# Layer 0 of a two-layer graph attention kernel: h and gate as one 512-column product in fifteen steps

## The chip, the cores and the metric

The kernel runs on one core of a Trainium2 chip. The metric is the device time of one execution in microseconds; the median of the runs counts. All data are 32-bit floats, and the products are made on TensorE (PE) in that type. The other engines are VectorE (DVE), ScalarE (ACT), GpSimd (POOL) and SyncE (SP), whose queue issues every load and store.

## The reference

The input is 128 graphs of 64 nodes with 768 features, and an adjacency mask. Two attention layers follow each other, each with a residual and a layer normalization. The change is in layer 0:

```python
h = einsum('bnd,ade->bane', x, W)              # 12 heads of 64: one 768 x 768 product
th = tanh(h)
attn = (th @ w_src) + (th @ w_dst).T           # per head, a 64 x 64 score of each graph
attn = where(attn >= 0, attn, 0.2 * attn); attn = where(~adj, -999, attn); attn = softmax(attn)
feat = elu(attn @ h + b)
gate = sigmoid(x @ H_w.T + H_b)                # a second 768 x 768 product
x1 = layernorm(x + gate * feat + (1 - gate) * x)
```

Layer 1 is a multi-head attention over x1 with four 768 x 768 products, for queries, keys, values (v) and the output.

## The kernel before

Tokens lie in 64 tiles of 128 (two graphs each), which go through the kernel in 32 pairs. Phase A (`phase_a`) is layer 0 together with the v product of layer 1; phase B is the rest of layer 1.

**Products.** Phase A multiplies a pair by a 768 x 768 matrix with a seven-product scheme: the pair, and the weights, are seen as 2 x 2 blocks of 384, and seven products of blocks (and of sums of blocks) do what eight would. The class `Product` (its matmuls are recorded at L214) does one such product in 7 steps of 3 matmuls, each with 128 x 128 of transposed tokens as the stationary side and 384 weight columns as the moving side. Its three accumulators X, Z and Y are banks of the pool `psX`, which has four. They are evicted partly by an ACT copy (`snap`, L444) and a DVE addition (`into`, L467), partly by a copy alone (L465). The sums of token blocks are four POOL instructions of 384 columns (`token_sums`, L263 to L266), those of weight blocks are made once at the start (`weight_sums`, L178). H_w is transposed at the start by PE (`hw_blocks`, L395).

Phase B uses another scheme for its products, with fifteen steps: 2 x 3 blocks of tokens by 3 x 3 blocks of 256 weights, fifteen products in place of eighteen. The table `STEPS` says for each step which token block or sum and which weight slot it takes, into which of four accumulator chains it goes, and to which of the six output blocks the running sum of the chain is added or subtracted after that step. The class `Stream` (L915) executes a step: two matmuls, and then the reads, the first of a block by `first` and later ones by `add`.

**Stages of a pair.** For a pair, phase A loads x twice (as rows, and as 32 x 32 blocks that DVE transposes, L423), makes h (`start_h`) and gate (`start_g`), and then for each of its two tiles: tanh (L504), a multiplication by w_dst on POOL (L508) and its sum per head on DVE (L511), the same for w_src (L516, L520), the w_dst scores to DRAM and back as rows (`dst_out`, `dst_in`), the other graph's h to the other partitions (`exchange`), scores with Prelu on ACT (L558), mask (L565) and maximum (L569) on DVE, Exp on ACT (L574), scaling on POOL (L584), transposing and aggregating on PE (L595, L613), ELU (`elu`), the mix with the gate (`mix1`, `mix2`: L646, L647, L655, L656), the normalization, and a store of x1. The gate's bias is added by POOL (`gate_in`, L623). Three pairs later x1 comes back, is transposed, and v is made with the third weight matrix.

**Order.** The order of the work is written out by hand: `at(step, f)` puts a piece of work at a step, and `run` issues the steps in order. Each engine executes its instructions in the order of issue. `O[p]` is the step at which pair p's h begins. It is 14 steps per pair for the first pairs, which have no v beside them, and 21 from then on: 7 for h, 7 for gate, 7 for v. A tile's other stages are placed at constants after `O[p]`.

**Weights.** W, H_w and Wv lie with their sums in three tiles, `w0`, `w1` and `w2`. When layer 0 is through, Wq and Wk are loaded into the places of `w0` and `w1`.

Of the kernel before, what the change touches and what calls it, by code (L numbers as in the profile page):

```python
# [20 lines left out]
BIG = 3e38  # L21

# [39 lines left out]
def kernel(  # L62
# [81 lines left out]
    def weight_tile(tag):  # L144
        return wts.tile([P, 7, CH, HALF], F32, name=f"w{tag}", tag=f"w{tag}")
# [3 lines left out]
    def weight15(i):  # L149
        t = wts.tile([P, 7, CH, HALF], F32, name=f"w{i}", tag=f"w{i}").rearrange(  # L150
            "p s c o -> p (s c o)"
        )

        spare[i] = t[:, 15 * 2 * 256 :]
        return t[:, : 15 * 2 * 256].rearrange("p (s c o) -> p s c o", s=15, c=2)
# [98 lines left out]

    PLACE = [(0, 0), (1, 1), (1, 0), (0, 1)]
# [4 lines left out]
    def token_sums(Ss, Ta, Tb):  # L260

        tt = nc.gpsimd.tensor_tensor
        tt(Ss[:, 0], Tb[:, :CH], Tb[:, CH:], ALU.add)  # L263
        tt(Ss[:, 1], Ss[:, 0], Ta[:, :CH], ALU.subtract)
        tt(Ss[:, 2], Ta[:, :CH], Tb[:, :CH], ALU.subtract)
        tt(Ss[:, 3], Ta[:, CH:], Ss[:, 1], ALU.subtract)  # L266

    def run(events, n_steps):
        for g in range(n_steps):
            for f in events.pop(g, []):  # L270
                f()
        assert not events, sorted(events)
# [56 lines left out]
    def phase_a(ctx):  # L329
        k6 = ctx.enter_context(tc.tile_pool(name="k6", bufs=2))  # L330
# [13 lines left out]
        hp = k3.tile([P, 3, D], F32, name="hp")  # L344
        gp = k3.tile([P, 3, D], F32, name="gp")
        h_at = [xb[:, 2], xb[:, 3], hp[:, 0], hp[:, 1], hp[:, 2]]
        g_at = [xb[:, 4], gp[:, 0], gp[:, 1], gp[:, 2]]
# [10 lines left out]
        def load_tile(p, i):  # L358
# [6 lines left out]
        w0 = weight_tile(0)  # L365
        w0_v = w0.rearrange("p s c o -> p s (c o)").rearrange(
            "p s (a c e) -> p s a c e", a=A // 2, e=E
        )
        W_v = W.rearrange("a (h p c) e -> h p a c e", h=2, c=CH)
        for kh, oh in ((0, 0), (1, 0), (0, 1), (1, 1)):  # L370
            nc.sync.dma_start(
                w0_v[:, SLOT[kh, oh]],
                W_v[kh][:, oh * 6 : (oh + 1) * 6],
            )

            if (kh, oh) == (1, 0):
                load_tile(0, 1)
        load_adj(0)
        w1 = weight_tile(1)
        hrows = {}  # L380

        def load_hrow(oc):

            if oc < 3:
                hrows[oc] = gp[:, oc]
            else:
                hrows[oc] = k3.tile([P, D], F32, name=("z", "tmp", "th")[oc - 3])
            nc.sync.dma_start(hrows[oc], H_w[oc * P : (oc + 1) * P, :])

        def hw_blocks(oc):  # L390
            hrow = hrows.pop(oc)
            for kh in range(2):
                ps = psa.tile([P, CH, P], F32, name="pa")
                for c in range(CH):
                    nc.tensor.transpose(ps[:, c, :], chunk0(hrow, kh * CH + c), ident)  # L395
                dst = w1[:, SLOT[kh, oc // CH], :, (oc % CH) * P : (oc % CH + 1) * P]
                nc.scalar.copy(dst, ps)

        for oc in range(NC):
            load_hrow(oc)  # L400
        wd_bc = rows(k3, w_dst.rearrange("a e o -> (a e o)"), "wd_bc")
        ws_bc = rows(k3, w_src.rearrange("a e o -> (a e o)"), "ws_bc")
        b_bc = rows(k3, b, "b_bc")
        hb_bc = rows(k3, H_b, "hb_bc")
        w2 = weight_tile(2)
# [41 lines left out]
        def sums(d):  # L447
            Ss = k6.tile([P, 4, CH, P], F32, name="S")
            token_sums(Ss, *d["T"])
            d["S"] = Ss  # L450
# [9 lines left out]
        def into(tiles):  # L460
            def sink(k, ps, kept):
                i, half = PLACE[k]
                o = tiles[i][:, halves(half)]
                if kept is None:
                    nc.scalar.copy(o, ps)  # L465
                else:
                    nc.vector.tensor_tensor(o, ps, kept, ALU.add)  # L467

            return sink

        def start_h(d):
            d["h"] = [h_at[(2 * d["p"] + i) % 5] for i in range(2)]
            d["W"] = product(d, lambda i, c: w0_v[:, i, :, c, :], into(d["h"]))

        def start_g(d):
            d["g"] = [g_at[(2 * d["p"] + i) % 4] for i in range(2)]
            d["G"] = product(d, lambda i, c: w1[:, i, c, :], into(d["g"]))
# [17 lines left out]
        class Tile0:  # L495
# [5 lines left out]
            def tanh(self):  # L501
                self.h = self.d["h"][self.i]
                self.th = k3.tile([P, D], F32, name="th")
                nc.scalar.activation(self.th, self.h, AF.Tanh)  # L504

            def dst_mul(self):
                self.tmp = k3.tile([P, D], F32, name="tmp")
                nc.gpsimd.tensor_tensor(self.tmp, self.th, wd_bc, ALU.mult)  # L508
# [112 lines left out]
            def gate_in(self):  # L621
                self.g = self.d["g"][self.i]
                nc.gpsimd.tensor_tensor(self.g, self.g, hb_bc, ALU.add)  # L623
# [5 lines left out]
            def elu(self):  # L629

                self.z = k3.tile([P, D], F32, name="z")
# [54 lines left out]

        for c in range(CH):
            at(0, lambda c=c: weight_sums(lambda s: w0_v[:, s, :, c, :], nc.vector, range(3)))

            at(1, lambda c=c: weight_sums(lambda s: w0_v[:, s, :, c, :], nc.vector, [3]))  # L690
            for k in range(4):
                at(
                    13 + 4 * c + k,
                    lambda c=c, k=k: weight_sums(lambda s: w2[:, s, c], nc.gpsimd, [k]),
                )
        for oc in range(NC):
            at(oc // 2 + 2, lambda oc=oc: hw_blocks(oc))

        for k, block in enumerate(((0, 0), (1, 0), (0, 1), (1, 1))):
            at(2 + k, lambda block=block: weight_plain(w2, Wv, [block]))  # L700
# [3 lines left out]


        O = [14 * p if p < 3 else 21 * p - 21 for p in range(NP)]
        for p in range(NP):
            d, o = st[p], O[p]
            d["p"] = p
            if p:  # L710
                at(max(o - 20, 1), lambda p=p: load_adj(p))
                at(o + 10, lambda p=p: load(p))
# [7 lines left out]
            if p:  # L720
                at(max(o - 20, 1), lambda d=d: xb_in(d, 0))
                at(max(o - 16, 1), lambda d=d: xb_in(d, 1))
                at(o - 6, lambda d=d: xT(d, 0))
                at(o - 5, lambda d=d: xT(d, 1))
                at(o - 4, lambda d=d: sums(d))
            else:
                at(0, lambda d=d: d.update(T=[transposed(d["x"][0])]))
                at(1, lambda d=d: d["T"].append(transposed(d["x"][1])))
                at(1, lambda d=d: sums(d))
            at(o, lambda d=d: start_h(d))  # L730
            at(o + 7, lambda d=d: start_g(d))
            for i in range(7):
                at(o + i, lambda d=d, i=i: dense(d, "W", i))
                at(o + 7 + i, lambda d=d, i=i: dense(d, "G", i))
            for i, s in ((1, o), (0, o + (4 if p == NP - 1 else 5))):
                t = Tile0(p, i)
                at(s + 6 + (i == 0), t.tanh, t.cap)
                at(s + 7, t.dst_mul)
                at(s + 8, t.src_mul)
                at(s + 9, t.dst_sum, t.dst_out)  # L740
                at(s + 10, t.src_sum)
                at(s + 13, t.dst_in)
                at(s + 16, t.exchange)

                at(s + (15 if i else 17), lambda t=t: t.add(0))
                at(s + (16 if i else 17), lambda t=t: t.add(1))
                at(o + (14 if i else 16), t.gate_in)
                at(o + (17 if i else 18), t.gate)
                n = s - (i == 1)
                at(n + 18, t.mask, t.top)  # L750
                at(n + 19, lambda t=t: t.exp(0))
                at(n + 20, lambda t=t: t.exp(1))
                (at_front if i else at)(s + 21, lambda t=t: t.scale(0), lambda t=t: t.scale(1))

                n = s - (p == NP - 1 and i == 1)
                at(n + 24, t.probs)
                at(n + 25, t.aggregate)
                at(s + 26, t.elu)
                at(s + 27, t.mix1)
                at(s + 28, t.mix2)  # L760
                at(s + 29, t.norm1)

                n = s + (0 if p == NP - 1 else 1)
                at(n + 30, t.norm2)
                at(n + 31, t.spill)
# [8 lines left out]
            def x1_sums(d):  # L774
                d["T"] = [d["x1T", i] for i in range(2)]
                sums(d)

            if p < NP - 3:
                v = O[p + 3] + 14
                times = ((1, v - 19, v - 13), (0, v - 16, v - 10))  # L780
            elif p < NP - 1:

                v = O[-1] + (21 if p == NP - 3 else 28)
# [503 lines left out]
```

## Time and profile before

| | us |
|---|---|
| median of 3 runs | 2845.72 (2845.65 to 2846.51) |
| span of the profiled execution | 2842.6 |
| end of phase A (the last v matmul ends) | about 1462 |
| DVE busy, share of the span | 65% |
| POOL busy, share of the span | 54% |
| ACT busy, share of the span | 42% |
| HBM read and written | 191.4 and 101.1 MB |

The profile is one execution. Its span goes from the first to the last instruction; the time of a run has some 3 us around it. Busy shares are averages over the two phases, so stages must be looked at for themselves. A matmul of 32-bit floats appears as two records in the trace, each with a weight load beside it. A busy PE says that its queue was full; how long a matmul takes is read from the distance between records in an unbroken stretch.

### The profile page before, as it was taken

The page shows a single profiled execution, that of the slowest core. Times are in us where ns is not written, and L with a number is a line of the kernel's source. Part 1 is how long each engine was busy: PE and PEld are TensorE (multiplying, and loading weights), DVE is VectorE, ACT ScalarE, POOL GpSimd, SP SyncE. Part 2 cuts the span into 40 slices and gives each one's busy share as a digit, 9 for nine tenths or more (in the row PEclk, how much of TensorE's full clock was granted, in tenths as well). Part 3 has the DMA queues.
Part 4 walks back from the last instruction along what each step waited for, and adds up shares of the span by engine and source line. Part 5 has one row for each costly group of instructions (what it writes and reads, how often), then busy time and mean ns, then how long its engine had stood idle before and what let it go on. Part 6 is the DMA issues. An engine that isn't in the chain of part 4 may idle for free.

```text
span 2842.6 us, 50750 instructions
## 1 busy us (share of the span) xinstructions
PE 2805.4 (99%) x18108; PEld 2062.4 (73%) x18108; DVE 1856.1 (65%) x3724; ACT 1199.2 (42%) x3737; POOL 1544.7 (54%) x1653
## 2 busy tenths in 40 slices
PE   8899999999999999999999999999999999999998
PEld 5556565655655656656568888888888888888887
DVE  4887777877878777777774555555555555555556
ACT  4666656566565665656632221222211222211223
POOL 4755656556566555665546545446555456454455
PEclk9999999999999999999999999999999999999999
DMA  5434444344454454544651221212211212211222
GB/s 168 118 115 143 138 136 143 116 139 143 132 146 120 133 151 124 146 126 132 183 186 35 90 71 63 81 58 89 90 66 62 87 57 90 89 64 63 90 84 73
DMA packets 358685, 308.41 MB, mean 108 GB/s; under 512 B 226593, under 2 KB 304161, under 8 KB 358433
## 3 DMA queue, kind: packets, MB, share of 16 engines
q1 hardware_dynamic: 358144, 304.77, 35.2%
q8 instruction: 144, 2.36, 0.4%
q14 instruction: 109, 0.88, 0.1%
q10 hardware_dynamic: 288, 0.39, 0.0%
HBM read 191.41 MB, written 101.06 MB: 103 GB/s over the span
## 4 chain that ended last, share of the span: by engine, by line
PE 91%; DVE 4%; ACT 1%; DMA 1%; POOL 1%; issue 1%; SPq 1%; DVEq 0%; POOLq 0%; ACTq 0%
PE X L915 43%; PE X L214 40%; PE pb L1062 2%; PE pb L980 2%; PE pa L613 2%; PE pa L595 1%; PE pb L1038 1%; DMA s<-dst_d 1%; ACT s L558 0%; POOL Sc L897 0%; ACT s L574 0%; DVE s L565 0%; DVE xb L656 0%; DVE z L646 0%; DVE T L423 0%
## 5 line engine op out<-in xcount | busy, mean ns | idle before, releaser
L214 PE MATMUL X<-w,S 128*128 128x384 f32 x2304 | 796.8, 491 | 10.9 <-DVE v L486 3.1
L214 PEld LDWEIGHTS X<-w,S 128*128 128x128 f32 x2304 | 430.3, 190 | 298.1 <-DVE v L486 4.3
L915 PE MATMUL X<-S,w 128*128 128x256 f32 x2752 | 635.4, 379 | 0.0
L214 PE MATMUL X<-w,T 128*128 128x384 f32 x1728 | 598.6, 489 | 7.4 <-ACT snap L444 6.4
L915 PEld LDWEIGHTS X<-S,w 128*128 128x128 f32 x2752 | 518.1, 190 | 68.0
L214 PEld LDWEIGHTS X<-w,T 128*128 128x128 f32 x1728 | 325.3, 191 | 234.6 <-ACT snap L444 18.5
L958 DVE TENSOR_TENSOR xs<-xs,X 128x256 f32<-128x256 f32 x512 | 209.7, 418 | 175.1 <-PE X L915 167.0
L915 PE MATMUL X<-w,Sc 128*128 128x256 f32 x1280 | 294.4, 381 | 0.1
L574 ACT ACTIVATE s<-s,nmx 128x64 f32<-128x64 f32 x768 | 256.1, 335 | 76.7 <-DVE nmx L569 76.7
L941 DVE TENSOR_TENSOR k<-k,X 128x256 f32<-128x256 f32 x320 | 132.6, 418 | 232.0 <-PE X L915 160.3
L915 PEld LDWEIGHTS X<-w,Sc 128*128 128x128 f32 x1280 | 241.5, 190 | 34.2 <-DVE xs L958 0.9
L941 DVE TENSOR_TENSOR q<-q,X 128x256 f32<-128x256 f32 x320 | 133.0, 419 | 193.4 <-PE X L915 153.9
L915 PE MATMUL X<-xb,w 128*128 128x256 f32 x1024 | 258.0, 382 | 0.4 <-ACT q L936 0.4
L326 ACT ACTIVATE xs<-xs,shift,rstd 128x768 f32<-128x768 f32 x62 | 63.5, 1025 | 436.5 <-POOL shift L322 430.2
L444 ACT COPY snap<-X 128x384 f32<-128x384 f32 x288 | 135.5, 470 | 226.8 <-PE X L214 224.3
L936 ACT ACTIVATE k<-X,bk_c 128x256 f32<-128x256 f32 x192 | 91.0, 474 | 316.1 <-PE X L915 316.1
L508 POOL TENSOR_TENSOR tmp<-th,wd_bc 128x768 f32<-128x768 f32 x64 | 147.8, 2310 | 124.7 <-ACT th L504 124.7
L915 PEld LDWEIGHTS X<-xb,w 128*128 128x128 f32 x1024 | 192.0, 190 | 27.9 <-ACT q L936 0.8
L558 ACT ACTIVATE s<-s,src 128x64 f32<-128x64 f32 x768 | 193.1, 335 | 32.8 <-DMA s<-dst_d 32.8
L936 ACT ACTIVATE q<-X,bq_c 128x256 f32<-128x256 f32 x192 | 91.0, 475 | 273.6 <-PE X L915 273.6
L897 POOL TENSOR_TENSOR w<-cT 128x256 f32<-128x256 f32 x32 | 23.3, 727 | 333.9 <-PE X L915 332.7
L317 POOL TENSOR_TENSOR rstd<-rstd,neg_half 128x1 f32<-128x1 f32 x126 | 69.1, 549 | 232.5 <-DVE rstd L316 232.1
(123 smaller groups left out, 4283.2 us busy)
## 6 DMA issues: line engine op xcount, KB each, us to landing
xb<-in_x_dram SPq DMA_DIRECT2D x64, 384.0 KB
s<-dst_d SPq DMA_DIRECT2D x128, 192.0 KB
x_d<-xb SPq DMA_DIRECT2D x64, 384.0 KB
xT_d<-T SPq DMA_DIRECT2D x64, 384.0 KB
v_d<-v SPq DMA_DIRECT2D x128, 192.0 KB
xb<-xT_d SPq DMA_DIRECT2D x32, 768.0 KB
xb<-v_d SPq DMA_DIRECT2D x256, 96.0 KB
xs<-x_d SPq DMA_DIRECT2D x64, 384.0 KB
```

The costliest lines, as they stand in the source:

```text
L214: nc.tensor.matmul(o, self.lhsT(i, c), rhs, start=first and c == 0, stop=last and c == CH - 1, skip_group_check=True,)
L317: nc.gpsimd.tensor_tensor(rstd, rstd, neg_half, ALU.pow)
L326: nc.scalar.activation(r, r, AF.Identity, bias=shift, scale=rstd)
L444: nc.scalar.copy(t, ps)
L508: nc.gpsimd.tensor_tensor(self.tmp, self.th, wd_bc, ALU.mult)
L558: nc.scalar.activation(self.s[:, a], self.s[:, a], AF.Prelu, bias=self.src[:, a : a + 1], alpha=LEAKY_ALPHA,)
L574: nc.scalar.activation(self.s[:, a], self.s[:, a], AF.Exp, bias=self.nmx[:, a : a + 1], accum_out=self.sm[:, a : a + 1],)
L613: nc.tensor.matmul(self.pos[h2][own, j, :], self.pt[rws, j, own], rhs, start=True, stop=True,)
L915: nc.tensor.matmul(ps, self.lhsT(r, slot, c), self.rhs(r, slot, c), start=start and c == 0, stop=stop and c == 1, skip_group_check=True,)
L936: nc.scalar.activation(o[:, b], ps, AF.Identity, bias=bias[:, hd : hd + 1], scale=1.0 if positive else -1.0)
L941: nc.vector.tensor_tensor(o[:, b], o[:, b], ps, ALU.add if positive else ALU.subtract)
L958: nc.vector.tensor_tensor(o, o, ps, ALU.add if positive else ALU.subtract)
```

## The change

The h and gate products become one product `HG` for most pairs. The weights of both lie side by side in `whg`: fifteen slots of two 128-row chunks with 512 columns, 256 of W and 256 of H_w. A `Stream`, which moves to the top of the kernel, does the fifteen steps for both at once; its accumulators have 512 columns. At the first read of an output block, DVE takes the gate's half, with its bias, and ACT takes h's half; later reads are one DVE addition over both halves.

```diff
+        def start_hg(d, key, parts):
...
+            def first(b, positive, ps):
+                o, ps = at_block(b), view(ps)
+                m = n
+                if lo + n == 2 and HB_EVICT:
+                    nb = b % 3
+                    hb = hb_bc[:, nb * 256 : (nb + 1) * 256]
+                    if positive:
+                        nc.vector.tensor_tensor(o[:, n - 1], ps[:, n - 1], hb, ALU.add)
+                    else:
+                        nc.vector.tensor_tensor(o[:, n - 1], hb, ps[:, n - 1], ALU.subtract)
+                    m = n - 1
+                if m:
+                    nc.scalar.activation(
+                        o[:, :m], ps[:, :m], AF.Identity, scale=1.0 if positive else -1.0
+                    )
+
+            def add(b, positive, ps):
+                o = at_block(b)
+                nc.vector.tensor_tensor(o, o, view(ps), ALU.add if positive else ALU.subtract)
...
             def gate_in(self):
-                self.g = self.d["g"][self.i]
-                nc.gpsimd.tensor_tensor(self.g, self.g, hb_bc, ALU.add)
+                self.g = self.d["hg"][self.i][:, 1]
+                if not HB_EVICT:
+                    nc.gpsimd.tensor_tensor(self.g, self.g, hb_bc, ALU.add)
```

The eleven sums of token blocks are POOL instructions of 256 columns, each in its own buffer:

```diff
+        S1 = [k1.tile([P, 2, P], F32, name=f"S{k}") for k in range(len(SUMS))]
...
+        def block_sum(d, k, eng):
+            r0, r1, op = SUMS[k]
+            eng.tensor_tensor(S1[k], block(d, r0), block(d, r1), op)
```

Pairs 0 and 1 are multiplied plainly, so that they need no sums of weights. Pair 0's h reads W as it is loaded (384 columns at a time), pair 1's h and both gates read blocks of 256 columns, in six matmuls for each block of a tile. ACT spreads W into `whg` (`spread_w`), and `hw_blocks` puts the transposed H_w there; the blocks that a weight sum will overwrite are kept a second time (`kept_at`).

```diff
+        def plain(d, i, half):
+
+            ps = psX.tile([P, HALF], F32, name="X")
+            for k in range(NC):
+                nc.tensor.matmul(
+                    ps.rearrange("p (a e) -> p a e", e=E),
+                    d["T"][i][:, k, :],
+                    w_raw[:, k // CH, half * 6 : (half + 1) * 6, k % CH, :],
+                    start=k == 0,
+                    stop=k == NC - 1,
+                    skip_group_check=True,
+                )
+            (nc.scalar.copy if half else nc.vector.tensor_copy)(d["hg"][i][:, 0, halves(half)], ps)
...
+        def plain_g(d, i, nb):
+
+            ps = psX.tile([P, 256], F32, name="X")
+            for k in range(NC):
+                slot, c = 3 * (k // 2) + nb, k % 2
+                nc.tensor.matmul(
+                    ps,
+                    d["T"][i][:, k, :],
+                    kept_at(slot)[:, c, :] if slot in KEPT else whg[:, slot, c, WH[1]],
...
+        W_ORDER = (1, 4, 5, 0, 8, 2, 3, 6, 7, 9, 10, 11, 12, 13)
...
+        for n, k in enumerate(W_ORDER):
+            at(BEGIN["sums"][n], lambda k=k: weight15_sum(whg, k, nc.vector, slice(0, 512)))
+        for k, part in enumerate(((0, 0), (1, 0), (0, 1), (1, 1))):
+            at(BEGIN["wv"][k], lambda part=part: weight_plain(w2, Wv, [part]))
```

The last pair takes the fifteen steps twice, first for h and then for the gate, with 256 columns. A full pair now has 22 steps, 15 for `HG` and 7 for v, and v comes two pairs behind. Steps are fractions now; a table gives each stage its place (`A_LEAD` for the tile that comes first, `A_TAIL` for the other, `A_PAIR` for the pair's loads and sums), and a long table `MOVED` of corrections is added for the first five and the last three pairs.

```diff
+O_FIRST = (0, 12, 34, 56)
...
-        O = [14 * p if p < 3 else 21 * p - 21 for p in range(NP)]
+        O = list(O_FIRST) + [O_FIRST[-1] + 22 * (p + 1) for p in range(NP - len(O_FIRST))]
+        END = O[-1]
+        V_BASE = O[2:] + [END + 21, END + 30]
...
+            if p < 2:
+                at(0, lambda d=d: places_hg(d))
+                for n in range(6):
+                    i = (n // 3 + p) % 2
+                    if first and n < 4:
+                        at(BEGIN["h0"][n], lambda d=d, n=n: plain(d, n // 2, n % 2))
+                    if p:
+                        at(BEGIN["h1"][n], lambda d=d, i=i, n=n: plain_blocks(d, i, n % 3))
+                    at(BEGIN[f"g{p}"][n], lambda d=d, i=i, n=n: plain_g(d, i, n % 3))
+                dense = []
+            elif last:
+                dense = [("W", o, 0.5, (0,)), ("G", o + 7.5, 0.5, (1,))]
             else:
...
+                dense = [("HG", o, 1, (0, 1))]
...
+            v = V_BASE[p] + 15 + V_MOVED.get(min(p, p - NP, key=abs), 0)
             at(v, lambda d=d: start_v(d))
```

Wq and Wk are loaded at later steps of the last pair, since `whg` lies in both of their places until its last product is done. Phase B is otherwise as before.

## The prediction

> **What bounds the kernel now.** First the page: which engine is full, and whether it stays full.
>
> ```profile
> span 2842.6 us, 50750 instructions
> PE 2805.4 (99%) x18108; PEld 2062.4 (73%) x18108; DVE 1856.1 (65%) x3724; ACT 1199.2 (42%) x3737; POOL 1544.7 (54%) x1653
> ...
> PE   8899999999999999999999999999999999999998
> ...
> PEclk9999999999999999999999999999999999999999
> ```
>
> TensorE is busy in every slice but the first two and the last, at its full clock. A busy PE need not be an efficient one, so I asked next for busy time by stage (PE, PEld, DVE, ACT, POOL, then clock, DMA share, GB/s).
>
> ```profile
> 0.00:50.00 50.00, 39.37 (x135) 24.52 (x136) 25.36 (x43) 13.73 (x27) 13.35 (x17) 0.97 0.70 209
> 50.00:100.00 50.00, 46.08 (x239) 26.90 (x238) 37.23 (x55) 35.73 (x135) 41.40 (x34) 1.00 0.39 95
> 100.00:150.00 50.00, 43.67 (x275) 25.57 (x274) 39.50 (x59) 34.95 (x129) 34.51 (x31) 0.97 0.41 112
> 150.00:200.00 50.00, 46.56 (x285) 27.72 (x284) 43.34 (x67) 32.07 (x108) 30.74 (x29) 0.97 0.42 121
> ...
> 300.00:500.00 200.00, 200.00 (x1059) 120.07 (x1058) 149.06 (x234) 128.14 (x460) 114.82 (x111) 1.00 0.48 140
> 500.00:700.00 200.00, 199.31 (x1056) 119.86 (x1055) 153.85 (x239) 120.97 (x410) 115.60 (x109) 1.00 0.44 129
> ...
> 1400.00:1450.00 50.00, 45.95 (x245) 27.55 (x244) 34.91 (x61) 26.20 (x97) 19.94 (x22) 1.00 0.76 243
> ```
>
> From 200 to 1400 us PE has no gap; 24.3 us are idle before 200 us (10.6, 3.9, 6.3, 3.4) and 4.1 us at the end of layer 0. The chain of waits gives the pitch.
>
> ```profile
> 134.16 9.70 PE X L214 x24
> ...
> 195.05 29.22 PE X L214 x90
> ...
> 227.72 7.94 PE X L214 x24
> ...
> 239.11 29.22 PE X L214 x90
> ...
> 1514.60 2.95 PE pb L980 x96
> ...
> 1579.96 37.32 PE X L915 x172
> ```
>
> One pair of token tiles takes 239.11 - 195.05 = 44.06 us of PE work. A matmul is recorded twice (4032 records of L214 for 32 x 3 products of 21 matmuls). A record of 384 columns takes 29.22/90 = 0.3247 us, one of 256 takes 37.32/172 = 0.217. The time goes with the columns, about 0.1077 us per 128, so I take 0.4324 us for 512, a width this trace doesn't have. Work taken from PE is therefore taken from the time, as long as the others keep up.
>
> **The change on PE.** A pair's h and gate are now 2 x 7 steps x 3 matmuls of 384: 84 records x 0.3247 = 27.27 us. Fifteen steps x 2 matmuls of 512 are 60 x 0.4324 = 25.94. That is 1.33 us a pair, for pairs 2 to 30: -38.6. The last pair's two separate fifteen-step products are 120 x 0.217 = 26.04: -1.2. Pair 0 plainly is 48 x 0.3247 + 72 x 0.217 = 31.21, pair 1 is 144 x 0.217 = 31.25: +3.9 and +4.0. **PE's work: -31.9 us.** The v product, transposes and aggregation keep their counts.
>
> **The change on the others**, from these rows (mean ns after "us,"):
>
> ```profile
> L958 DVE TENSOR_TENSOR xs<-xs,X 128x256 f32<-128x256 f32 x512 | 209.7, 418 | 175.1 <-PE X L915 167.0 <-POOL xs L879 3.0
> ...
> L623 POOL TENSOR_TENSOR gp<-gp,hb_bc 128x768 f32<-128x768 f32 x48 | 87.7, 1839 | 0.0
> ...
> L467 DVE TENSOR_TENSOR gp<-X,snap 128x384 f32<-128x384 f32 x80 | 44.0, 551 | 8.7 <-PE X L214 5.3 <-ACT s L558 3.3
> ```
>
> *DVE* had (149.06 + 153.85)/400 x 44.06 = 33.4 us a pair. Six evictions of 0.55 go (3.3). Ten additions of 512 columns come; from 418 and 551 ns I extend to 686: 6.9 us. Six first evictions of 256 with the gate's bias come: 2.5. So 39.5 of a new pair of 44.06 - 1.33 = 42.7 us, 92%. *POOL* loses the bias, 2 x 1.84, and 4 sums of about 1.1 us; it gets 11 of 0.73 (the 256-wide sums of L897): 8.0 for 8.1, nothing. *ACT* loses 8 copies of 0.47 and gets 6 of 0.47: -0.9. None of this is on PE's path by its sum; only its place in a queue can matter. If that cover failed and DVE became the bound, its 8% of air is 3.2 us a pair.
>
> **Where a queue can bite.** A chain's running sum is read after each step, and the chain's next matmul comes two steps later: 2 x 4 x 0.4324 = 3.46 us for the read. I walked one pair through the changed kernel's instruction order with the rows' durations. The tightest place follows the tail of the previous pair, at the lead tile's aggregation (end: A). DVE has queued there: two z additions (0.93, counting start to start), the other tile's mask (1.10) and maximum (0.87), the gate's first read of step 11 (0.42), a wait for ACT's first read of h (0.55 with its signals), the 512-wide addition (0.6). It ends at A + 4.6; PE wants that bank for step 14 at A + 3 x 1.73 = 5.2. Then mix1 and mix2 stand ahead of the read of step 12, done at A + 7.1, while v's second step wants that bank at A + 8.9. Both fit, the first by 0.6 us. The mask waits for the Prelus, these for a DMA; behind it are PE's banks. From a stall of nothing to 0.5 us a pair I take 0.1: **+3** (0 to +15).
>
> Two rules of the Trainium skill speak against the change. *SBUF — State Buffer*, section "Who interferes with whom": a VectorE operation with two SBUF inputs and a GpSimd one that reads SBUF lock each other out for the whole instruction. The timeline shows it:
>
> ```profile
> 499.72 0.95 DVE L655 SCALAR_TENSOR_TENSOR z<-gp,z 128x768 f32<-128x768 f32 x1
> ...
> 509.53 2.57 POOL L508 TENSOR_TENSOR tmp<-th,wd_bc 128x768 f32<-128x768 f32 x1 [1.94 <-ACT th L504]
> ...
> 510.82 2.10 DVE L655 SCALAR_TENSOR_TENSOR z<-xb,z 128x768 f32<-128x768 f32 x1
> ```
>
> 0.95 alone, 2.10 behind POOL. If each pair's mask met such a lock, 1.15 - 0.6 = 0.55 us would reach PE, +16 in all. But POOL's queue has nothing ready between the x1 sums, done about when the aggregation is, and the scalings, which wait for the exponentials; so I take the uncontended values. *PSUM — Partial Sum Buffer*, "PSUM bank collisions raise a hardware error": two engines must not read one bank of the same partitions at once. Here the first read of each block is split between DVE and ACT in one bank; the order does make ACT wait for DVE. In parallel the pair would take 0.47, in turn 0.42 + 0.47 + signals = 1.0. No row of before has it; it is in the walk above, inside the 3.46 us.
>
> **The start.** Before, PE loses 24.3 us of idle plus a slow clock: 9.70 against 7.94 for 24 records at 134 us, and 4.18 us for the first six (0.70 each): together 28.3. It waits there for the weight sums (DVE needs W, then 12 and 12 sums) and for pairs that follow at 14 steps each. Now the plain products need no sums. By the rows: 5.9 for x, 0.6 for its copy, 2.2 cold, 0.7 for W's second half, whose landing moves from third to fourth in SP's queue. Then 13 us of h, the H_w transposes, and h of pair 1, whose x blocks are no longer followed by Wv in the queue; they land at about 27 us (6.7 + 0.8 MB at 0.35 MB/us from 5 us, rates of the first 30 us), turned at 28.4, wanted at 28.7. The 14 weight sums of 1024 columns (about 1.2 us each, by the 684 ns of a 512-wide DVE sum, L290, extended) lie beside 31 us of gate products. Pair 2 then meets DVE late by about 1.4 us, and POOL with 12 sums of Wv at 1.05 (L178) on top of its own work, perhaps 2; 3.5 for what I missed. That makes 16: **-12** (-17 to 0, if every saved wait returns at pair 2).
>
> **The end.** v of pair 31 needs the last tile's softmax. Before, three v products cover it (13.6 us each), now two, and the last one is held back behind the tail's transposes. The hole, by the same chain (two DMA trips, Prelu, Exp, scaling), is about 5 us at the transposes and 1 behind, against 4.1: **+2** (-1 to +8). Wq's and Wk's loads come later but 15 us ahead of use: nothing.
>
> **Sum.** -31.9 - 12 + 2 + 3 = -38.9. The profiled execution has a span of 2842.6; the median of the runs, 2845.7, is 3.1 above it, which I keep: 2842.6 - 38.9 + 3.1 = **2806.8, say 2807**. By this sum alone, with its unknown costs at their ends, 2798 to 2815.
>
> **Rivals.**
> *DVE gives part back* (25%): a stall of 0.3 to 1.0 us at step 14 in each of 29 pairs. For it: 92% load, 0.6 us of margin; against: DVE catches up with PE by step 9 in the walk. At 0.6 us: 2807 + 14 = 2821.
> *The start gains nothing* (9%): pairs 0 and 1 cost 7.9 more and pair 2 waits. For it: POOL at 41.40 of 50 us already in 50 to 100. 2819.
> *Slower* (8%): the mask waits for the tail tile's dst rows. Their DMA is issued behind four block loads, and ends in the walk only just ahead of ACT's Prelu; ACT's copies for the aggregation, and DVE's reads of PE's banks, stand behind these. For it: before, the mask already idles 64 us over 64 times for Prelus and DMAs; against: nothing of PE's stood behind it then. Its margin is about 1.6 us; beyond that each us costs 29. From about 3 us late in every pair the gain is gone; at 3.6 us, 2 x 29 more than taken: 2807 + 58 = 2865.
> *512 columns are not in proportion* (1%): at 0.455 a record the step saves nothing, about 2846. The straight line through 256 and 384 speaks against it.
> The forecast itself has 57%.
>
> Within 0.2% (5.7 us) one can't tell a change from none: same 3%, between the rivals; slower 7%; faster 90%. The range for eight in ten reaches past the forecast's own into the first rival: 2796 to 2829.
>
> **What would show it.** Right: records of 512 columns at about 0.43 us; pairs 42.7 us apart; DVE near 92% and PE without gaps from pair 3 to 30; PE's idle before 200 us near 14. Wrong: PE gaps released by DVE's additions at step 14, or by ACT's copies ahead of the aggregation, once a pair; a mask that idles for Prelus more than 1.6 us; idle at the end above 10 us. What would make the forecast wrong most easily is a wait that is small but comes in all 29 pairs.

## The result, and the profile after

The changed kernel takes 2820.86 us (median of 4 runs, 2816.27 to 2822.24), the kernel before, run beside it, 2846.11 us (2845.65 to 2847.83). The ratio is 0.9907, with a 95% interval of 0.9893 to 0.9921: 25 us faster, where 39 were forecast. The profiled execution has a span of 2820.1 us, 22.5 below the 2842.6 of before; single executions scatter by a few us, so the spans need not differ by what the medians do.

The page of the changed kernel, with busy time, PE's busy share in 40 slices, and the granted clock:

```profile
span 2820.1 us, 50020 instructions
...
PE 2775.9 (98%) x17544; PEld 1958.7 (69%) x17544; DVE 1905.0 (68%) x4026; ACT 1163.1 (41%) x3685; POOL 1495.9 (53%) x1791
...
PE   8899999999999999999799999999999999999998
...
PEclk9999999999999999999899999999999999999999
```

There is a new dip, in PE's row and in its clock, at the twentieth slice (1339 to 1410 us), shortly before phase A ends at 1436 us. Busy time by stage, in the columns of before (PE, PEld, DVE, ACT, POOL, then clock, DMA share, GB/s):

```profile
0.00:50.00 50.00, 42.09 (x181) 31.95 (x182) 12.14 (x22) 24.50 (x68) 7.94 (x10) 1.00 0.61 175
50.00:100.00 50.00, 43.66 (x263) 32.44 (x262) 42.69 (x69) 25.78 (x92) 20.50 (x24) 0.97 0.41 119
100.00:150.00 50.00, 46.46 (x214) 23.08 (x214) 42.43 (x65) 23.22 (x81) 34.61 (x40) 0.96 0.41 122
150.00:200.00 50.00, 50.00 (x233) 25.52 (x232) 40.93 (x72) 33.00 (x128) 31.37 (x38) 1.00 0.52 149
300.00:500.00 200.00, 200.00 (x971) 103.10 (x970) 164.46 (x289) 123.05 (x438) 118.02 (x142) 1.00 0.49 142
...
1300.00:1400.00 100.00, 85.81 (x520) 54.93 (x519) 75.50 (x139) 63.83 (x243) 49.61 (x56) 0.95 0.53 151
1400.00:1450.00 50.00, 44.98 (x195) 29.08 (x194) 35.55 (x69) 13.01 (x34) 13.43 (x13) 0.89 0.63 205
```

The chain of waits in the steady part gives the pitch and the record:

```profile
245.41 7.07 PE X L428 x16
...
267.74 17.17 PE X L428 x40
...
288.13 7.06 PE X L428 x16
```

The reader sees three things. The middle is as forecast: no idle time in 300 to 500 us, a pitch of 288.13 - 245.41 = 42.72 us, 17.17/40 = 0.429 us for a record of 512 columns. The start loses 17.8 us of idle time before 200 us (7.9 + 6.3 + 3.5), against 24.3. The end of phase A loses 19.2 us (14.2 + 5.0), against 4.5. Records also run slower than their width allows, at half speed for a few microseconds after an idle stretch; summed over these records this is about 9 us at the start of before and none at its end, about 6 and 7 us now. The span's 22.5 us then come apart like this:

| term | forecast | measured | from |
|---|---|---|---|
| PE's work | -31.9 | about -32 | pitch; time of a record x count |
| the middle's stalls | +3 | about -4 | below |
| start: idle and slow clock | -12 | -9 (33 to 24) | 24.3 + 9 to 17.8 + 6 |
| end: idle and slow clock | +2 | +22 (4.5 to 26) | 4.5 to 19.2 + 7 |
| sum | -38.9 | -23 | span: -22.5 |

The middle's -4: between the evictions of v of pairs 4 and 26 the old trace has 972.3 us, 44.19 a pair, not the 44.06 of the stretch that the forecast took its pitch from; the new one has 939.9, 42.72 a pair. The change saves 1.47 us a pair there, 0.14 x 29 = 4 us more than the forecast reckoned. Single pairs of before take between 44.06 and 45.19 us: its middle had small stalls, where the forecast read none (its row for 500 to 700 us has PE busy for 199.31 of 200).

So two questions are open: why the start gains less, and what fails at the end.

### The profile page after: what moved, and what is told of

The parts are those of the page before. It is cut to its first block, busy times and chain, and to the rows that moved or that the text cites. A ratio compares the mean times of both kernels' runs of the same rounds, so it can differ in the third digit from the quotient of the medians.

```text
span 2820.1 us, 50020 instructions
## 1 busy us (share of the span) xinstructions
PE 2775.9 (98%) x17544; PEld 1958.7 (69%) x17544; DVE 1905.0 (68%) x4026; ACT 1163.1 (41%) x3685; POOL 1495.9 (53%) x1791
## 4 chain that ended last, share of the span: by engine, by line
PE 93%; DVE 3%; DMA 1%; POOL 1%; ACT 1%; SPq 0%; issue 0%; POOLq 0%; DVEq 0%; ACTq 0%
PE X L428 70%; PE X L373 15%; PE pa L901 2%; PE pb L1326 2%; PE pb L1244 2%; PE pa L883 1%; PE pb L1302 1%; PE X L715 1%; PE X L700 1%; POOL Sc L1190 0%; DMA w<-in_L_gnn_Wv_dram 0%; DVE s L853 0%; ACT s L862 0%; DMA hb_bc<-in_L_gnn_H_b_dram 0%; DVE T L634 0%
## 5 line engine op out<-in xcount | busy, mean ns | idle before, releaser
L428 PE MATMUL X<-S,w 128*128 128x256 f32 x2752 | 636.5, 380 | 0.0
L428 PE MATMUL X<-w,S 128*128 128x512 f32 (+1 forms) x1364 | 598.9, 584 | 10.7 <-POOL S L668 7.5
L428 PEld LDWEIGHTS X<-S,w 128*128 128x128 f32 x2752 | 519.1, 190 | 68.5
L428 PEld LDWEIGHTS X<-w,S 128*128 128x128 f32 x1364 | 254.9, 191 | 289.8 <-issue 241.0
L872 POOL TENSOR_TENSOR s<-s,rs 128x384 f32<-128x384 f32 x128 | 106.9, 836 | 372.1 <-DVE rs L870 355.9
L428 PE MATMUL X<-w,Sc 128*128 128x256 f32 x1280 | 294.4, 381 | 0.1
L373 PE MATMUL X<-w,S 128*128 128x384 f32 x768 | 270.9, 490 | 1.5 <-POOL S L456 1.4
L428 PEld LDWEIGHTS X<-w,Sc 128*128 128x128 f32 x1280 | 241.5, 190 | 34.1 <-DVE xs L1222 0.9
L428 PE MATMUL X<-xb,w 128*128 128x256 f32 x1024 | 258.6, 383 | 0.8 <-ACT q L1200 0.8
L428 PE MATMUL X<-w,T 128*128 128x512 f32 (+1 forms) x496 | 223.9, 583 | 5.7 <-DVE xb L757 3.4
L428 PEld LDWEIGHTS X<-xb,w 128*128 128x128 f32 x1024 | 192.2, 190 | 28.4 <-ACT q L1200 1.2
L757 DVE TENSOR_TENSOR hgp<-hgp,X 128x512 f32<-128x512 f32 (+1 forms) x235 | 150.6, 651 | 80.8 <-PE X L428 67.2
L373 PEld LDWEIGHTS X<-w,S 128*128 128x128 f32 x768 | 141.1, 190 | 90.1 <-POOL S L456 1.6
```

What stands on the lines that cost most here:

```text
L373: nc.tensor.matmul(o, self.lhsT(i, c), rhs, start=first and c == 0, stop=last and c == CH - 1, skip_group_check=True,)
L428: nc.tensor.matmul(ps, self.lhsT(r, slot, c), self.rhs(r, slot, c), start=start and c == 0, stop=stop and c == 1, skip_group_check=True,)
L757: nc.vector.tensor_tensor(o, o, view(ps), ALU.add if positive else ALU.subtract)
L872: nc.gpsimd.tensor_tensor(t, t, rs[:, :, None].to_broadcast([P, A // 2, S]), ALU.mult)
```

## The experiments

**Theory at the start.** Two waits of PE stand out in the timeline of the changed kernel (in brackets: idle time before the instruction, and who ended it).

```profile
95.98 5.40 PE L428 MATMUL X<-w,S 128*128 128x512 f32 x8 [4.62 <-POOL S L668]
...
120.19 3.42 PE L428 MATMUL X<-w,T 128*128 128x512 f32 x4 [3.37 <-DVE xb L757]
```

POOL's own timeline tells why the first came:

```profile
89.63 1.81 POOL L796 TENSOR_TENSOR w<-th,wd_bc 128x768 f32<-128x768 f32 x1
93.53 0.99 POOL L337 TENSOR_TENSOR w<-w 128x384 f32<-128x384 f32 x1 [2.08 <-DMA w<-in_L_gnn_Wv_dram]
94.49 2.12 POOL L668 TENSOR_TENSOR S<-T 128x256 f32<-128x256 f32 x2
```

A sum of Wv's blocks (L337) stands at the head of POOL's queue until Wv has landed; pair 2's token sums (L668) need nothing of Wv and stand behind it. For the second wait, DVE's mask at 111.83 us takes 5.85 us, where 0.95 is usual:

```profile
111.83 5.85 DVE L853 TENSOR_TENSOR s<-s,cap 128x768 f32<-128x768 f32 x1
```

*The Wv sums late.* Only the places of three sums change:

```diff
-"v_sums": (34.44, 37, 38, 40.19, ...
+"v_sums": (38.4, 38.6, 38.8, 40.19, ...
```

> The first three sums of Wv blocks on POOL come after all token sums of pair 2, nothing else is changed. Theory (POOL's queue stands at the first Wv sum until Wv has landed, with pair 2's token sums behind it): PE's 4.6 us wait for POOL's S in pair 2 falls below 1.5 us, the slow clock behind it (1.9 us) goes too, and the time falls by 3 to 6 us, to about 2815 to 2818. The DVE mask of 5.85 us at 111.8 us stays, since POOL's run of sums stays. Rival (pair 2 is limited by DVE and POOL's own work, whatever the order): another wait of 4 us takes its place and the time stays within 1 us of 2821.

Measured: 2813.91 us (2811.22 to 2818.24), ratio 0.988 (0.9865 to 0.9895) against the before of its own chip, 2848.21; against the change's 0.9907 that is 0.0027, 7.7 us. The timeline of this kernel at the same places:

```profile
91.71 3.70 PE L428 MATMUL X<-w,S 128*128 128x512 f32 x8 [0.84 <-POOL S L668]
```

```profile
106.61 1.21 DVE L853 TENSOR_TENSOR s<-s,cap 128x768 f32<-128x768 f32 x1
```

POOL's wait fell from 4.62 to 0.84 us, and the records behind it run at full speed. Idle time before 200 us is 12.0 us, slow records cost about 3. The start's loss is 15 us, and the forecast had put it at 16. The theory holds; the rival, another wait in its place, does not. One part of the expectation was wrong: the long mask went too, although POOL's run of sums stayed.

*The Wv sums on DVE.*

```diff
-weight_sums(lambda s: w2[:, s, c], nc.gpsimd, [k])
+weight_sums(lambda s: w2[:, s, c], nc.vector, [k])
```

The places are those of the late sums.

> The twelve sums of Wv blocks are made by DVE instead of POOL, at the same late steps. Theory (the 5.85 us mask is DVE locked out by an unbroken run of POOL instructions): the mask falls to 1.1 to 2 us, PE's 3.4 us wait for DVE's addition behind it goes, together with the POOL wait the time falls by 6 to 10 us, to 2811 to 2815. Rival (DVE is the bound of pair 2): 12 x 0.5 = 6 us more on DVE show as PE waits for L757 of at least 4 us in 95 to 125 us, and the time is no better than with the sums late on POOL.

Measured: 2814.98 us (2814.3 to 2816.1), ratio 0.9883 (0.9868 to 0.9897), no better than the late sums on POOL. The mask takes 1.45 us, and PE's waits for L757 are 0.8 and 0.3 us. The theory's numbers came, the time at the edge of its range, but they don't speak for it: the late sums alone, on POOL, give the same, and there was no lock left to remove. The rival's waits of 4 us did not come; DVE takes the twelve sums without becoming the bound. What the start lacked is lost by the order in POOL's queue, and by a lock that came with it.

**Theory at the end.** The waits of PE from 1320 to 1450 us in the changed kernel (total, times, longest):

```profile
PE pa L883 <- POOL s L872: 6.5, 4, 2.3
PE X L428 <- DVE hgp L757: 4.0, 3, 1.9
PE X L428 <- POOL S L668: 2.7, 1, 2.7
PE X L428 <- ACT xs L1437: 1.7, 1, 1.7
PE X L373 <- POOL S L456: 1.4, 1, 1.4
PE pa L901 <- DMA hx<-hgp: 1.1, 1, 1.1
```

L883 and L901 are the transposes of the softmax and the aggregation: with 0.3 us for an ACT copy, 7.9 us are lost there. L428 with `S` and `hgp` are the last pair's own products: 6.7 us. The last two tiles' work is a set of short pieces in five queues. The first theory was that pieces stand in the wrong order; the first rival, that the loads of Wq and Wk, now later, are in the way of the score rows and the exchange (the DMA engines are 0.92 busy from 1390 to 1410 us).

*Wq and Wk later.* `SEAM["wq"]` goes from 15.2 to 21.41 to steps 33.4 to 34.4, `SEAM["wk"]` from 23.61 to 31.16 to steps 35 to 36.

> All loads of Wq and Wk move behind the last exchange and x1 load (steps 33 to 36 of the last pair). Theory (the hole before the last tile's transposes is the order of work in the in-order queues of ACT, DVE and SP): PE's waits at the transposes stay at 6 to 7 us, only the 1.1 us for the exchange shrinks; time within 2 us of 2821. Rival (the DMA traffic of Wq and Wk, 4.7 MB at a share of 0.92, delays the score rows and the exchange): the waits at transposes and aggregation fall from 7.9 to below 4 us and the time by 4 us or more, or it is given back at the seam if Wq then lands too late.

Measured: 2820.73 us (2816.18 to 2822.55), ratio 0.9898 (0.9881 to 0.9914). The waits at transposes and aggregation are 5.7 + 1.2 + 1.1 = 8.0 us. They are not due to these loads. A new wait of 3.1 us, for a DVE read of v, came shortly before phase B: DVE stands 6.5 us at a sum of phase B's first tokens (L480), whose load from `xT` now follows those of Wq and Wk, and the read of v stands behind it. The giving back that the rival allowed for is there, its gain is not.

*Three pieces in another order.* The last pair's token sums 4 to 10 go ahead of step -0.49, where pair 29's normalization stands; in addition:

```diff
-(-1, "lead", "exchange", None): 0.56
+(-1, "lead", "exchange", None): -2.5
-(-1, "lead", "elu", None): 0.56
+(-1, "lead", "elu", None): 1.1
```

> Three moves in the last pair: its last seven token sums stand ahead of pair 29's normalization on POOL; its lead tile's exchange stands ahead of pair 30's store of x1 on SP; its tail tile's second six Exp stand ahead of the lead tile's ELU Exp on ACT. Theory (order in the queues): PE's 2.7 us wait for S at 1339 us goes, the 1.1 us wait for the exchange goes, the waits at the tail's transposes fall from 4.4 to about 2.5 us; time 4 to 7 us lower, 2814 to 2817. Rival (the last pair is limited by DVE's and ACT's work as a whole): the waits reappear elsewhere in 1330 to 1410 us, PE's idle there stays near 16 us, time within 1.5 us of 2821.

Measured: 2819.65 us (2818.59 to 2821.58), ratio 0.99 (0.9885 to 0.9914). The wait for S went, with 1.15 us of a DVE wait in its place, and so did that for the exchange. But the waits at the transposes grew from 6.5 to 10.6 us. DVE's timeline shows what came in between:

```profile
1388.62 1.26 DVE L634 STREAM_TRANSPOSE T<-xp 128x384 f32<-128x384 f32 x2 [2.32 <-DMA xp<-x_d]
1389.80 0.15 DVE L870 RECIPROCAL rs<-sm 128x6 f32<-128x6 f32 x1
```

The reciprocal for the last lead tile's second scaling stands behind a transposition that waits for a DMA. Latency changed its place: the rival was nearer.

*All moves together.* The late Wv sums, the three moves above, that transposition behind the last mask (`(-2, "pair", "x1T1")` from 1.69 to 3.4), and the tail's second scaling ahead of the lead's mix (`(-1, "tail", "scale1")` from -0.02 to -0.39).

> The start's edit (Wv sums behind pair 2's token sums) together with the three moves in the last pair, and two more that the trace of those moves asks for: DVE's transposition of pair 30's first x1 tile, which waits for a DMA, stands behind the last pair's mask instead of ahead of the lead tile's second scaling, and the tail tile's second scaling stands ahead of the lead tile's mix. Theory: the start gives 8 us as before, the last pair 4 us in its products (S) and 2 to 4 us at the transposes (waits 10.6 to about 6 us); 2806 to 2811 us. Rival (the last pair's latencies only change places): no better than the start's edit alone, 2813 to 2815 us.

Measured: 2810.22 us (2809.29 to 2813.58), ratio 0.9873 (0.9859 to 0.9888). This is faster than both kernels, the fastest of the study. Against the late sums alone (0.988) the intervals overlap. The traces say the rest: from the last pair's first matmul to phase B's first, the changed kernel takes 100.0 us (1335.6 to 1435.6), the late sums 99.4, this one 97.5. The start gives most of it: the last pair begins 8.5 us earlier than in the changed kernel.

*One product as wide as the others for the last pair.*

```diff
-dense = [("W", o, 0.5, (0,)), ("G", o + 7.5, 0.5, (1,))]
+dense = [("HG", o, 1, (0, 1))]
```

The tiles' stages move with it, and v of pair 31 and the weight sums by 7 steps.

> The last pair too takes h and gate as one 512-column product; its tiles' stages and what follows them stand 7 steps later. Theory (the last pair's 256-column steps halve the time that a read has: 3.46 us becomes 1.74, so queues that were hidden show): the 6.7 us of PE waits for S and for DVE's additions inside the last pair's products fall below 1.5 us, but h ends 13 us later and the wait ahead of the last tile's transposes grows by up to 12 us, since only v products that are ready can cover it; in sum +0 to +8 us against 2821. Rival (the waits come from how much DVE and ACT have to do there, not from the step's width): the waits inside the product stay at 5 us or more.

Measured: 2836.44 us (2835.59 to 2841.99), ratio 0.9969 (0.9958 to 0.998). The waits from 1320 to 1366 us, which hold the product (this kernel's lines are two higher: L430 for L428, L885 for L883, L651 for L649):

```profile
PE pa L885 <- POOL s L874: 1.7, 1, 1.7
PE X L430 <- DVE hgp L759: 0.3, 1, 0.3
```

and from 1366 to 1470 us:

```profile
PE pa L885 <- POOL s L874: 12.6, 2, 10.7
PE pa L651 <- DVE xb L956: 8.8, 1, 8.8
PE pa L903 <- DMA hx<-hgp: 4.5, 1, 4.5
PE pa L903 <- ACT pt L890: 4.5, 2, 4.2
```

The 6.7 us inside the products came down to 0.3: they belong to the 256-column step, which leaves a read 2 x 4 x 0.217 = 1.74 us, half of what 512 columns leave. But h is ready later, and everything behind it waits: some 15 us more in all, twice what was allowed for. Taking h alone first is dear inside the product and cheap outside it.

*A product that nobody reads, as cover.* 21 matmuls of 384 columns (13.6 us of PE, the size of one v product) are added. First between the last gate product and v of pair 29:

```diff
+def fill(i):
+    ps = psX.tile([P, HALF], F32, name="X")
+    for c in range(CH):
+        nc.tensor.matmul(
+            ps, st[NP - 1]["T"][i % 2][:, c, :], w2[:, i, c, :], start=c == 0, stop=c == CH - 1
+        )
+for i in range(7):
+    at(O[-1] + 14.6 + 0.01 * i, lambda i=i: fill(i))
```

> 21 matmuls of 384 columns that nobody reads (13.6 us of PE at full clock, as much as one v product) are put between the last pair's gate product and v of pair 29. Theory (the hole at the last transposes is latency of the last two tiles' softmax, one v product short of cover): PE's 7.9 us of waits at the transposes and the aggregation go to below 2 us and the slow clock behind them goes, so that the 13.6 us cost only 2 to 6 us. Rival (the last tiles' softmax is held up by PE's own order, or by the v products' evictions on ACT and DVE, and moves along): the waits stay and the time rises by 11 to 14 us.

Measured: 2831.69 us (2828.16 to 2833.73), ratio 0.9943 (0.9926 to 0.9959); from the last pair's first matmul to phase B it takes 109.0 us, 9.0 more. The waits at transposes and aggregation are 5.7 + 1.3 + 1.1 = 8.1 us, as before. The hole moved along: the rival. Behind the fill on PE stands pair 30's tail aggregation; DVE's read of it stands ahead of the last pair's mask in DVE's queue, and v's evictions stand between the Exp on ACT.

Then the same work behind v of pair 29 (step 23.05, reading pair 29's tiles), and the last lead tile's transposes, aggregation and ELU behind the tail tile's Exp:

```diff
-(-1, "lead", "probs", None): 0.56
+(-1, "lead", "probs", None): 1.68
-(-1, "lead", "aggregate", None): 0.56
+(-1, "lead", "aggregate", None): 1.47
-(-1, "lead", "elu", None): 0.56
+(-1, "lead", "elu", None): 1.3
```

The tail's second scaling moves by -0.37 too.

> The same 21 matmuls that nobody reads (13.6 us of PE) stand now behind v of pair 29, and the last lead tile's transposes, aggregation and ELU stand behind the tail tile's Exp on ACT, so that nothing of the tail's softmax waits for PE. Theory (the hole at the last transposes is latency that a product could cover, but only where no copy or read of PE's work stands ahead of the softmax in ACT's and DVE's queues): the waits at transposes and aggregation fall from 7.9 to below 3 us, the slow clock behind them goes, and the fill costs 3 to 6 us instead of the 9.6 that it cost ahead of v. Rival (the hole follows PE wherever the fill stands): waits stay near 8 us, cost 9 to 13 us.

Measured: 2825.87 us (2823.61 to 2828.99), ratio 0.993 (0.9913 to 0.9946), and 107.7 us for the stretch. PE's waits from 1382 to 1440 us in this kernel:

```profile
PE X L373 <- DVE T L634: 2.5, 1, 2.5
PE pa L883 <- POOL s L872: 2.4, 2, 2.2
PE X L373 <- ACT T L650: 0.3, 1, 0.3
PE pa L901 <- ACT pt L888: 0.2, 1, 0.2
```

Transposes and aggregation wait 2.6 us in place of 7.9, and slow records cost 2 to 3 us in place of 7. The hole can be covered. The 7.7 us by which the stretch grew are more than the 3 to 6 expected; a part of that is the new order itself: without the fill, and with the token sums early, it takes 103.1 us, as the next run shows. By the medians this run is only 5 us above the change, but not by its edit alone: its last pair begins 4.2 us earlier, since the long mask at the start did not occur in it (last section).

*That order without a fill*, with the late Wv sums and the early token sums.

> Start: Wv sums behind pair 2's token sums. Last pair: its last seven token sums ahead of pair 29's normalization on POOL, and the lead tile's transposes, aggregation and ELU behind the tail tile's Exp. No fill, no other move. Theory: start 8 us better than 2821, the last pair's products 2 to 4 us, the tail's transposes 1 to 3 us; 2806 to 2811 us. Rival (latencies change places): 2812 to 2815 us, as with the start's edit alone.

Measured: 2815.34 us (2813.99 to 2816.53), ratio 0.9889 (0.9874 to 0.9904). The start's gain is there, and the end gives part of it back: PE waits 3.9 us for the lead tile's copy, now behind twelve Exp. The rival.

*The tail's tanh earlier.*

```diff
-(-1, "lead", "src_sum", None): 0.56
+(-1, "lead", "src_sum", None): -0.69
+(-1, "tail", "tanh", None): -0.74, (-1, "tail", "dst_mul", None): -1.73
```

> As the run before, and in addition the last lead tile's w_src sum stands ahead of pair 30's second mix on DVE, which frees the buffer of the tail's tanh, whose tanh and w_dst multiplication come earlier. Theory (the tail's softmax starts late because its tanh waits for a buffer behind DVE's mixes): the tail's tanh starts about 2 us earlier after pair 30's mix, and the time is 1 to 3 us below the run before. Rival (ACT's two blocks of twelve Exp set the pace): no difference beyond 1 us.

Measured: 2815.39 us (2814.86 to 2817.99), ratio 0.9891 (0.9876 to 0.9906): no difference in time. The stretch shrank from 103.1 to 101.0 us, which the times don't show. Nothing is claimed from it.

**The middle: how near is DVE?** The forecast's walk had found 0.6 us of margin at step 14 of each pair. The tail tile's row maximum is repeated, without any effect on what is computed:

```diff
+dose = (self.p - 4) // 8 + 1 if self.i == 0 and 4 <= self.p < 28 else 0
+for _ in range(1 + dose):
     nc.vector.tensor_reduce(self.nmx, self.s, AX.X, ALU.max, negate=True)
```

> The tail tile's row maximum (0.95 us on DVE, just ahead of DVE's reads of PE's banks at the tightest place of the walk) is repeated: once more in pairs 4 to 11, twice in 12 to 19, three times in 20 to 27. By the walk of the prediction (0.6 us of margin at step 14): each pair loses 0.35, 1.3 and 2.25 us, PE shows gaps of 3, 10 and 18 us in the three stretches, +31 us in all. Rival (the margin is much larger, since DVE's collisions with POOL are shorter than before): no gap up to two repeats, and at most 1 us a pair at three; +0 to +8 us. Theory for the steady term of zero: the rival.

Measured: 2856.74 us (2852.8 to 2858.28), ratio 1.0031 (1.0018 to 1.0044), about 35 us above the change. The chain of waits, with the start of the same stretch of each pair (one, two and three repeats):

```profile
353.37 17.17 PE X L428 x40
...
396.44 17.17 PE X L428 x40
...
612.81 17.17 PE X L428 x40
...
656.87 17.17 PE X L428 x40
...
1104.83 17.17 PE X L428 x40
...
1149.88 17.17 PE X L428 x40
```

The pitch is 43.07, 44.06 and 45.05 us, against 42.72: 0.35, 1.34 and 2.33 us a pair, where the walk says 0.35, 1.3 and 2.25. The gaps stand at step 14, ahead of the matmuls that reuse the bank of the addition L757. The rival, on which the study had bet, fell; the walk's margin of 0.6 us holds to 0.1 us. There is no stall in the changed kernel because 0.6 us are left in every pair, and not because DVE has much room.

## Why the prediction was right and wrong

The measured 2820.9 us lies inside the wide range (2796 to 2829) and outside that of the sum itself (2798 to 2815). It is also the number that the first rival had, 2821; that is chance, for the stall that this rival names did not occur. The forecast was right in PE's work and in the mechanism of the middle, and wrong at the start and above all at the end; the middle came out 7 us better than forecast, which hides a part of what the end lost. A small error lies in its last line: each listed run is 1.8 us longer than its span (2821.93 and 2820.1), where the forecast added 3.1.

- **PE's work** was right: 0.429 us for 512 columns (0.432 taken), a pitch of 42.72 (42.7). The rival with 512 columns out of proportion is gone.
- **The middle** was right in its mechanism: the tightest place, its engine and its margin were those of the walk. The +3 that was added for safety was not there, and neither was the rival that made DVE the loser at step 14, nor the slower one with the mask behind late score rows: PE has no gap from 200 to 1300 us. The first read of a block, shared out between DVE and ACT, takes 0.8 us from the start of DVE's part to the end of ACT's (118.59 to 119.41 us), where about 1.0 was taken. The old pitch was read from one unbroken stretch; over 22 pairs it is 44.19, so the change saves 1.47 a pair and not 1.33.
- **DVE's load** was near: 164.46/200 x 42.72 = 35.1 us a pair, 82%, where 39.5 and 92% were reckoned. The additions of 512 columns take 0.67 us (0.686 taken); most of the difference is in the four instructions of the mix, which take 0.96 to 0.97 us on average, where the same four had 1.24, 1.00, 1.89 and 1.33 before: 3.2 us a pair. That they meet POOL's instructions less often is the likely reason; no run tested it.
- **The start** failed in a term of the sum, "POOL with 12 sums of Wv at 1.05 (L178) on top of its own work, perhaps 2". The durations were right (about 1.0 us a sum); the wait was left out. The first sum waits for a DMA at the head of the queue, with pair 2's token sums behind it: 4.6 us and the slow clock after it, and behind this a mask held up for 5 us and a wait of 3.4. With the three sums moved the start loses 15 us, and 16 were forecast. The gain is then 18 us and not the 12 of the forecast, for a second reason: the old start lost 33 us, where 28.3 were reckoned, since slow records were counted at two places only (4 us of 9).
- **The end** failed, and it is most of what is missing: the hole "about 5 us at the transposes and 1 behind", +2, against +22 measured. Three things were not in it. The last pair's own products stall for 6.7 us, since 256-column steps leave a read half the time; the walk was made for a full pair alone, and the last pair was costed by its PE work. The hole is 7.9 us in place of 6. And idle PE is slow afterwards: about 7 us. Phase B's first matmuls wait 2.5 us where 0.4 was seen before; what delays them was not sought.
- The forecast named "idle at the end above 10 us" as a sign of wrong, and it is what showed.

What stays open: what would bring the end back. The cover run shows that the hole is latency that PE work can hide, if no copy or read of that work stands ahead of the last softmax. The old order has one more v product there. Holding back one more in the new one needs room for its transposed tiles in SBUF, and was not tried; so that the missing v product is the whole cause is argued, not shown. The moves tried, without a fill or another product, left the stretch between 97.5 and 103.1 us.

## What to carry to other kernels

An instruction that waits for a load must be placed by when the load lands, and not only by when its engine has time: look at what needs nothing of that load and stands behind it in the same queue. When a schedule is checked by walking one steady round, walk the first and the last round too, with their own step lengths; a read that fits a step of 512 columns may not fit one of 256. And cost an idle stretch of PE with the slow records that follow it.

## What the runs showed of the hardware

**A mask locked out through several POOL instructions.** The long mask at 111.83 us stands beside this run of POOL instructions:

```profile
111.10 1.00 POOL L456 TENSOR_TENSOR S<-T 128x384 f32<-128x384 f32 x1
112.06 1.00 POOL L337 TENSOR_TENSOR w<-w 128x384 f32<-128x384 f32 x1
...
115.88 0.99 POOL L456 TENSOR_TENSOR S<-T,S 128x384 f32<-128x384 f32 x1
```

POOL goes on at a pitch of 0.96 us, and the mask ends 0.8 us after the last of the six, at 117.68. Seven traces have that order of the start. In six of them it took 5.1 to 6.6 us and ended about 0.8 us after a POOL instruction; in the seventh (the second fill) it took 1.24 us, and the next POOL instruction 1.72. PE's wait of 3.4 us for L757 is absent from that trace; so this wait comes from the lock. The Trainium skill (SBUF — State Buffer, "Who interferes with whom") has the lock between such instructions as exclusive, and lets whoever issues first hold the ports for the whole instruction (it says so of VectorE's two-port modes); here the turn did not change over several instructions. What decides it the runs do not show. It may be one reason why the changed kernel's times spread by 6 us (2816.27 to 2822.24) where those of before spread by 2; that was not tested.

**Half speed after waits of 1 to 3 us.** The granted clock of the changed kernel (the column before the last two) around the last pair's wait for `S` and around its last transposes, and records of each:

```profile
1338.00:1342.50 4.50, 1.84 (x9) 1.23 (x8) 2.95 (x7) 1.56 (x3) 4.03 (x6) 1.00 0.62 242
1342.60:1345.90 3.30, 3.27 (x8) 2.11 (x8) 0.35 (x1) 2.51 (x9) 3.29 (x4) 0.50 0.11 29
1393.80:1407.40 13.60, 7.78 (x62) 4.52 (x60) 9.68 (x13) 6.61 (x30) 6.32 (x6) 0.50 1.00 263
1407.50:1420.00 12.50, 12.50 (x89) 7.97 (x89) 10.34 (x21) 3.23 (x6) 1.63 (x3) 1.00 0.34 127
```

```profile
1341.90 3.56 PE L428 MATMUL X<-w,S 128*128 128x256 f32 x8 [2.66 <-POOL S L668]
...
1363.32 1.89 PE L428 MATMUL X<-w,S 128*128 128x256 f32 x8
...
1403.56 4.10 PE L373 MATMUL X<-w,T 128*128 128x384 f32 x6
...
1408.45 2.20 PE L373 MATMUL X<-w,T 128*128 128x384 f32 x6
```

A single wait of 2.66 us was followed by half the clock, and eight records of 256 columns took 3.56 us where 1.89 is usual. At the transposes the clock fell at 1393.8 us, after two waits of 1.05 us with 0.55 us of work between them, and stayed at half over two more waits of 2.2 us; six records of 384 columns took 4.10 us there, and 2.20 just behind. Behind the wait of 4.62 us eight records of 512 took 5.40 us where 3.70 is usual; behind single waits of 1.7 and 1.9 us nothing was slow. The skill (TensorE: Matmul & The Clock Gate, "Part 1: The HAM clock gate") has half the rate after an idle window of about 3.4 us; here shorter waits were enough. How idle PE must be for it the runs do not show.
